# Waits at the edges of a TensorE-bound kernel: load order, warm-up matmuls, halved products, copies on ScalarE, group ends over two pairs

## The chip, the cores and the metric

The kernel runs on one core of a Trainium2 chip. The metric is the device time of one execution in microseconds (us), as the median of several.

The engines are TensorE (PE, matmuls), VectorE (DVE), ScalarE (ACT), GpSimd (POOL) and SyncE (SP, which here only issues DMA). In the lines of a profile, L342 is line 342 of that kernel's source, so one statement has different numbers in different kernels. `a<-b` is output from input. A matmul of the source appears as two instructions.

## The reference

Two layers of a compressed interaction network over x of shape (4096, 32, 16), each followed by a batch norm over rows and embedding:

```python
def _cin_layer(out, x, W, b, gamma, beta):
    r, _, e = x.shape
    h = jnp.einsum('rne,rfe->rnfe', out, x).reshape(r, -1, e)
    h = jnp.einsum('rce,oc->roe', h, W) + b[None, :, None]
    return _batchnorm(h, gamma, beta)
h1 = _cin_layer(x, x, W1, b1, g1, beta1)          # 1024 -> 128 channels
out, direct1 = (h1[:, :64], h1[:, 64:])
direct2 = _cin_layer(out, x, W2, b2, g2, beta2)   # 2048 -> 128 channels
return jnp.concatenate([direct1, direct2], axis=1).sum(axis=-1)
```

## The kernel before

Layer 1 goes over 128 tiles of 512 columns. VectorE multiplies `a` and `b` of a tile to `z`, TensorE multiplies `z` by the weights in four matmuls. The diagonal leftovers (`zr`) of four tiles come in four matmuls ahead of them. ScalarE takes the sums out of PSUM (the memory that the matmuls write), and VectorE collects their statistics.

```python
for t in range(NT):
    s = t % GROUP
    if s == 0:
        r = load_rem(t // GROUP)
        zr = rpool.tile([P, T], FP, tag="zr", name="zr")
        nc.vector.tensor_tensor(zr, r[:, :T], r[:, T:], ALU.mult)
    a, b = load_main(t)
    z = zpool.tile([P, 2, 2, T], FP, tag="z", name="z")
    nc.vector.tensor_tensor(z, ...)
    ...
    with tc.issue_after(loads[-1].ins):
        for first, load in EARLY:      # x loads, differences, first loads of layer 2
            if t == first:
                early.append(load())
```

Layer 2 goes over 64 pairs of tiles, each in four stages: one ordinary stage first (16 matmuls), then three that use Strassen's scheme (14 matmuls each, at the price of additions on the operands). VectorE makes two products `zz` per stage, GpSimd forms the operands `t` of the Strassen stages in two operations, and the sums of a pair are combined during the next pair. After 20 pairs the statistics of a group are aggregated. The direct half of layer 1's output is scaled during the first pair:

```python
def write_direct():
    sum_direct(NC - 1)
    ...
    nc.vector.tensor_scalar(ss1[high, 2:3], ss1[high, 1:2], float(EMB), None, ALU.mult)
    for half in range(2):
        nc.vector.tensor_copy(direct[half * KEEP : (half + 1) * KEEP, :], ss1[high, 0:3:2])
    nc.scalar.activation(d1, d1, AF.Identity, scale=direct[:, 0:1], bias=direct[:, 1:2])
...
# in combine, which runs during the next pair:
    if idle:
        dve(idle.pop(0))
    add(e[:, 0], both, x62)
    ...
    if stats_x.ended():
        ends = [swap_groups, stats_y.aggregate]
        if c < NC - 1:
            idle[:0] = [lambda: [end() for end in ends][-1]]
```

Of the kernel before, what the change touches and what calls it, by code (L numbers as in the profile page):

```python
# [35 lines left out]
FP = mybir.dt.float32  # L36
AF = mybir.ActivationFunctionType
# [3 lines left out]
P = 128  # L41
# [13 lines left out]
PLAIN = 3  # L55
STAGES = (3, 0, 1, 2)
DIFF = 16


@with_exitstack  # L60
def tile_cin(ctx: ExitStack, tc: tile.TileContext, xa, xb, xr, w1, w1m, w2, bn, out):
# [2 lines left out]
    const = ctx.enter_context(tc.tile_pool(name="const", bufs=1))  # L64
    dram = ctx.enter_context(tc.tile_pool(name="dram", bufs=1, space=bass.MemoryType.DRAM))
    sums = ctx.enter_context(tc.tile_pool(name="sums", bufs=1))
    spool = ctx.enter_context(tc.tile_pool(name="spool", bufs=1))
    epool = ctx.enter_context(tc.tile_pool(name="epool", bufs=2))
    xpool = ctx.enter_context(tc.tile_pool(name="xpool", bufs=1))
    bpool = ctx.enter_context(tc.tile_pool(name="bpool", bufs=2))  # L70
# [15 lines left out]
    class Stats:  # L86
# [25 lines left out]
        def ended(self):  # L112
            return self.at == self.sizes[self.group]

        def aggregate(self):

            size = self.sizes[self.group]
            group = self.groups[:, self.group]
            stats = self.stats[:, :size].rearrange("p a b -> p (a b)")
            done = nc.vector.bn_aggr(group[:, 1:3], stats)  # L120
            if size != LAST:
                done = nc.vector.tensor_scalar(group[:, 2:3], group[:, 2:3], size / LAST, None, ALU.mult)
            self.at = 0
            self.group += 1
            return done

    def scale_shift(name, groups, gamma, beta, factor=None):

# [75 lines left out]
        return dict(zip(STAGES, a)), b, bx  # L204



    select = bpool.tile([KEEP, 4, 16, 8], FP, tag="b", name="select")
    nc.gpsimd.memset(select, 1.0)
# [19 lines left out]
    with ExitStack() as one:  # L229
# [6 lines left out]
        def load_rem(g):  # L236

            r = rpool.tile([P, 2 * T], FP, tag="r", name="r")
            nc.sync.dma_start(r, bass.AP(xr.tensor, xr.offset + g * P * 2 * T, [[2 * T, P], [1, 2 * T]]))
            return r  # L240

        def load_main(t):
# [8 lines left out]

        w1_sb = wpool.tile([P, 6, P], FP, tag="w1", name="w1_sb")
        nc.scalar.dma_start(w1_sb, w1)
        w1m_sb = lpool.tile([P, 6, P], FP, tag="a", name="w1m_sb")
        nc.scalar.dma_start(w1m_sb, w1m)
        bn_sb = load_bn()
        w2_sb = const.tile([P, 16, P], FP, tag="w2", name="w2_sb")
        s_sb = const.tile([P, 4, 4, 2, KEEP], FP, tag="s", name="s_sb")
        neg_sb = const.tile([P, 2, 2, KEEP], FP, tag="neg", name="neg_sb")
        nc.scalar.dma_start(w2_sb, w2)  # L260
        b1, g1, beta1, b2, g2, beta2 = (bn_sb[:, k : k + 1] for k in range(6))
        nc.vector.tensor_tensor(w1_sb, w1_sb, w1m_sb, ALU.add)

# [19 lines left out]
        def finish(t):  # L283

            c, half = divmod(t, 2)
            ps = pss.pop(t)
            to = slice(half * KEEP, (half + 1) * KEEP)
            if half == 0:
                eds[c] = epool.tile([P, T], FP, tag="ed", name="ed")
                kept[c] = opool.tile([KEEP, 2 * T], FP, tag="h", name="kept")  # L290
            ed = eds[c]
            if t == NT - 1:
                stats1.add(ps, b1)
            else:
                e = opool.tile([P, T], FP, tag="e", name="e")
                nc.scalar.activation(e, ps, AF.Identity, bias=b1)  # L296
                stats1.add(e)
            if stats1.ended():
                stats1.aggregate()
            h = kept[c]  # L300
            nc.scalar.activation(h[:, half * T : (half + 1) * T], ps[:KEEP, :], AF.Identity, bias=b1[:KEEP])
            if half == 1:
                nc.scalar.dma_start(hs[c], kept.pop(c))
            if t == NT - 1:
                return ps
            evict_direct(ed[to, :], ps)
            if half == 1:
                sum_direct(c)
# [9 lines left out]
                ALU.add,  # L318
            )

        zr = None
        for t in range(NT):
            s = t % GROUP
            if s == 0:
                r = load_rem(t // GROUP)
                zr = rpool.tile([P, T], FP, tag="zr", name="zr")
                nc.vector.tensor_tensor(zr, r[:, :T], r[:, T:], ALU.mult)
            a, b = load_main(t)
            z = zpool.tile([P, 2, 2, T], FP, tag="z", name="z")
            nc.vector.tensor_tensor(  # L330
                z,
                a.rearrange("p (a t) -> p a t", a=2).unsqueeze(2).to_broadcast([P, 2, 2, T]),
                b.rearrange("p (b t) -> p b t", b=2).unsqueeze(1).to_broadcast([P, 2, 2, T]),
                ALU.mult,
            )
            if s % 4 == 0:
                for k in range(4):
                    ps = pss[t + k] = psum.tile([P, T], FP, tag="ps", name="ps")
                    rows = slice(32 * k, 32 * (k + 1))
                    nc.tensor.matmul(ps, w1_sb[rows, 4 + s // 4, :], zr[rows, :], start=True, stop=False)  # L340
            for m in range(4):
                nc.tensor.matmul(pss[t], w1_sb[:, m, :], z[:, m // 2, m % 2, :], start=False, stop=(m == 3))  # L342
            if t > 0:
                finish(t - 1)
            if t == 8:
                combine_weights()
            with tc.issue_after(loads[-1].ins):
                for first, load in EARLY:
                    if t == first:
                        early.append(load())  # L350
# [4 lines left out]
    def keep_running(count):  # L355

        for k in range(count):
            nc.tensor.matmul(  # L358
                running, w2_sb[:, k, :], w2_sb[:, 0:4, :].rearrange("p a b -> p (a b)"), start=True, stop=True
            )  # L360
# [13 lines left out]
    nc.tensor.matmul(keep_ps, spread, blocks, start=True, stop=True)  # L374
    keep = const.tile([P, 4, 2], FP, tag="keep", name="keep")
    nc.vector.tensor_copy(keep, keep_ps)
    keep_running(2)

    with tc.issue_after(root1):
        evict_direct(eds[NC - 1][high, :], last)  # L380
# [1 line left out]
    def write_direct():  # L382
        sum_direct(NC - 1)
        direct = const.tile([P, 2], FP, tag="direct", name="direct")
        nc.vector.tensor_scalar(ss1[high, 2:3], ss1[high, 1:2], float(EMB), None, ALU.mult)
        for half in range(2):
            nc.vector.tensor_copy(direct[half * KEEP : (half + 1) * KEEP, :], ss1[high, 0:3:2])
        nc.scalar.activation(d1, d1, AF.Identity, scale=direct[:, 0:1], bias=direct[:, 1:2])
        for half in range(2):
            nc.scalar.dma_start(  # L390
                out[:KEEP, half * (ROWS // 2) : (half + 1) * (ROWS // 2)],
                d1[half * KEEP : (half + 1) * KEEP, :],
            )
# [8 lines left out]
    groups_of = -(-(NC - LAST) // SG) + 1  # L402
    groups2 = const.tile([P, 2, groups_of, 3], FP, tag="groups2", name="groups2")
    stats_x, stats_y = Stats("x", NC), Stats("y", NC, groups2[:, 0])

    def swap_groups():
        g = stats_x.group
        stats_x.aggregate()
        nc.vector.tensor_copy(groups2[low, 1, g], stats_x.groups[high, g])
        return nc.vector.tensor_copy(groups2[high, 1, g], stats_x.groups[low, g])  # L410

    b2_swapped = const.tile([P, 1], FP, tag="b2s", name="b2_swapped")
    nc.vector.tensor_copy(b2_swapped[low], b2[high])


    idle = []
    lasts = {}

    def queue(engine, make):
# [5 lines left out]
    def dve(make):  # L425
        return queue("dve", make)
# [7 lines left out]
    def multiply(z, a, b):  # L434

        a = a.unsqueeze(1).unsqueeze(1).to_broadcast([P, 2, 2, T])
        dve(lambda: nc.vector.tensor_tensor(z, a, b.rearrange("p (k q) t -> p k q t", k=2), ALU.mult))  # L437

    def factor(a, i, half):
        f = factors.tile([P, T], FP, tag="f", name="f")  # L440
# [21 lines left out]
            queue("pe", lambda: nc.tensor.matmul(self.of[x], w, b, start=start, stop=stop))  # L462

    def ordinary(sums_, z):
        for k in range(4):
            q = k % 2
            z1, z2 = z[:, 0 if k < 2 else 3, q], z[:, 2 if k < 2 else 1, q]
            a11, a21, a12, a22, s1, s2, s3, s4 = weights(PLAIN, q)
            sums_.matmul(3, s4 if k < 2 else neg_sb[:, 0, q], z2)
            sums_.matmul(2, a11 if k < 2 else a12, z1)  # L470
            sums_.matmul(5, s1 if k < 2 else neg_sb[:, 1, q], z2)
            sums_.matmul(4, a21 if k < 2 else a22, z1)
# [21 lines left out]
    def combine(c, sums_):  # L494
# [27 lines left out]
        dve(lambda: stats_x.add(e[:, 0]))  # L522
        dve(lambda: stats_y.add(e[:, 1]))
        if stats_x.ended():
            ends = [swap_groups, stats_y.aggregate]
            if c < NC - 1:
                idle[:0] = [lambda: [end() for end in ends][-1]]
            else:
                for end in ends:
                    dve(end)  # L530
        yield
        dve(
            lambda: nc.vector.tensor_reduce(
# [11 lines left out]
    for c in range(NC):  # L545
# [14 lines left out]
        for k, i in enumerate(STAGES):  # L560

            z = z2pool.tile([P, 4, 2, T], FP, tag="zz", name="zz")
            multiply(z[:, 0::3], f1, b)
            if k in (1, 2, 3):

                step()
            f2 = factor(raw[i], i, 1)
            if k == 1:
                step()
            multiply(z[:, 1:3], f2, bx)  # L570
            if k == 1:
                step()
            if k == 2:
                step()
            if k < 3:
                f1 = factor(raw[STAGES[k + 1]], STAGES[k + 1], 0)
            if k == 0:
                step(2)
            if k == 1:
                step()  # L580
            if i == PLAIN:
                ordinary(sums_, z)
            else:
                strassen(sums_, i, z, k == 3)
            if c == 0 and k == 1:
                with tc.issue_after(lasts["dve"].ins), tc.issue_after(lasts["act"].ins):
                    write_direct()
# [89 lines left out]
```

## Time and profile before

| | kernel before |
|---|---|
| time at hand for the prediction, median of 3 | 2136.95 us (2136.57 to 2137.31) |
| span of the profiled execution | 2135.7 us |
| TensorE busy | 98% |
| VectorE busy | 90% |
| first layer, 4 tiles, steady | 15.00 us |
| second layer, a pair, at best | 24.89 us |

With TensorE busy in all but 2% of the span, the page as a whole tells little. One reads the timelines of single stretches, from one matmul start to the next: 0.43 us is the fastest pace of the full matmuls (kernel before, from 19.17 us on), at which the array is called warm here, and 0.85 the pace of a cold one (there from 14.31 to 18.58 us). The prediction shows these lines.

### The profile page before, as it was taken

How to read it: one execution, taken by the hardware profiler on the slowest of the kernel's cores; microseconds unless marked ns; L12 is line 12 of the kernel's file. 1: busy time of each engine (PE TensorE's matmuls, PEld its weight loads, DVE VectorE, ACT ScalarE, POOL GpSimd, SP SyncE). 2: the span in 40 equal slices, each digit the busy share in tenths (PEclk: the TensorE clock that was granted, in tenths of full speed). 3: DMA queues.
4: the chain of work that ended last, by engine and by line, in shares of the span. 5: the costliest groups of instructions: out<-in, count | busy, mean ns of one | idle time of the engine just before them, and what ended most of it. 6: DMA issues, size and time to landing. Idle time of an engine off the chain costs nothing.

```text
span 2135.7 us, 23411 instructions
## 1 busy us (share of the span) xinstructions
PE 2091.2 (98%) x8716; PEld 733.8 (34%) x8716; DVE 1916.1 (90%) x1465; ACT 853.8 (40%) x1221; POOL 1328.5 (62%) x390
## 2 busy tenths in 40 slices
PE   7999999998999999999999999999999999999996
PEld 3344444443333333333333333333333333333332
DVE  7888888897999999989999998999999989999996
ACT  3555555554333333333333333333333333433332
POOL 0000000003878888887888888878888888788885
PEclk9999999999999999999999999999999999999998
DMA  9999999997767677777677777766667777666751
GB/s 355 332 341 335 333 338 351 356 353 197 189 166 171 167 185 175 171 173 171 158 175 180 174 172 173 174 166 159 167 169 173 172 174 174 163 166 160 171 135 40
DMA packets 112019, 440.65 MB, mean 206 GB/s; under 512 B 13088, under 2 KB 13088, under 8 KB 103456
## 3 DMA queue, kind: packets, MB, share of 16 engines
q1 hardware_dynamic: 105152, 416.33, 71.5%
q10 hardware_dynamic: 6752, 22.81, 2.9%
q8 instruction: 68, 1.11, 0.2%
q14 instruction: 47, 0.39, 0.1%
HBM read 417.07 MB, written 22.02 MB: 206 GB/s over the span
## 4 chain that ended last, share of the span: by engine, by line
PE 83%; POOL 8%; DVE 4%; issue 2%; DMA 2%; ACT 1%; SPq 0%; DVEq 0%; POOLq 0%
PE x L462 63%; PE ps L342 18%; POOL t L481 5%; POOL t L478 3%; DVE zz L437 2%; PE ps L340 1%; DVE z L330 1%; DMA b<-in_xb 1%; ACT both L429 0%; DMA x<-in_xb 0%; DMA a<-in_xa 0%; DMA r<-in_xr 0%; DVE e L432 0%; PE running L358 0%; DVE x L184 0%
## 5 line engine op out<-in xcount | busy, mean ns | idle before, releaser
L462 PE MATMUL x<-zz,w_sb 128*64 128x512 f32 x2560 | 968.9, 593 | 0.0
L478 POOL TENSOR_TENSOR t<-zz 128x1024 f32<-128x1024 f32 x192 | 456.8, 2379 | 770.7 <-DVE zz L437 770.7
L462 PE MATMUL x<-zz,s_sb 128*64 128x512 f32 x2048 | 924.8, 594 | 4.6 <-issue 4.6
L481 POOL TENSOR_TENSOR t<-zz,t 128x2048 f32<-128x2048 f32 x192 | 875.8, 4562 | 15.1
L462 PE MATMUL x<-t,s_sb 128*64 128x512 f32 x1536 | 696.4, 594 | 6.7 <-POOL t L481 6.5
L429 ACT ACTIVATE f<-a,keep 128x512 f32<-128x512 f32 x512 | 398.2, 778 | 634.0 <-DVE zz L437 631.3
L437 DVE TENSOR_TENSOR zz<-f,b 128x2048 f32<-128x2048 f32 x256 | 582.8, 2277 | 0.9 <-ACT f L429 0.8
L437 DVE TENSOR_TENSOR zz<-f,bx 128x2048 f32<-128x2048 f32 x256 | 582.5, 2275 | 0.1
L342 PE MATMUL ps<-z,w_sb 128*128 128x512 f32 x1024 | 451.1, 598 | 6.6 <-DVE z L330 6.6
L462 PEld LDWEIGHTS x<-zz,s_sb 128*64 128x64 f32 x2048 | 281.1, 137 | 372.0 <-issue 356.9
L462 PE MATMUL x<-t,w_sb 128*64 128x512 f32 x768 | 363.2, 595 | 0.0
L462 PEld LDWEIGHTS x<-t,s_sb 128*64 128x64 f32 x1536 | 205.1, 137 | 456.8 <-issue 397.5
L330 DVE TENSOR_TENSOR z<-a,b 128x2048 f32<-128x2048 f32 x128 | 292.9, 2288 | 56.7 <-DMA b<-in_xb 30.9
L462 PEld LDWEIGHTS x<-zz,w_sb 128*64 128x64 f32 x2560 | 301.3, 137 | 109.6 <-issue 106.4
L342 PEld LDWEIGHTS ps<-z,w_sb 128*128 128x128 f32 x1024 | 192.8, 191 | 263.4 <-issue 241.3
L462 PE MATMUL x<-zz,neg_sb 128*64 128x512 f32 x512 | 230.2, 592 | 0.0
L296 ACT ACTIVATE e<-ps,bn_sb 128x512 f32<-128x512 f32 x127 | 87.3, 688 | 245.7 <-PE ps L342 227.4
L432 DVE TENSOR_TENSOR both<-both,x 128x512 f32<-128x512 f32 x64 | 44.0, 688 | 130.4 <-ACT both L429 130.4
L429 ACT ACTIVATE u<-e,bn_sb 64x512 f32<-64x512 f32 x64 | 46.2, 722 | 192.3 <-DVE e L432 192.3
L462 PEld LDWEIGHTS x<-zz,neg_sb 128*64 128x64 f32 x512 | 70.1, 137 | 146.3 <-issue 146.3
L462 PEld LDWEIGHTS x<-t,w_sb 128*64 128x64 f32 x768 | 99.9, 137 | 0.0
L429 ACT ACTIVATE both<-x 64x512 f32<-64x512 f32 x64 | 38.1, 595 | 138.6 <-PE x L462 138.6
(70 smaller groups left out, 878.3 us busy)
## 6 DMA issues: line engine op xcount, KB each, us to landing
a<-h SPq DMA_DIRECT2D x256, 512.0 KB, 5.1
b<-in_xb SPq DMA_DIRECT2D x128, 512.0 KB, 6.9
a<-in_xa SPq DMA_DIRECT2D x128, 512.0 KB, 6.1
b<-in_xb SPq DMA_DIRECT2D x64, 1024.0 KB, 7.1
bx<-in_xb SPq DMA_DIRECT2D x64, 512.0 KB, 6.0
bx<-x SPq DMA_DIRECT2D x64, 512.0 KB, 7.7
h<-kept ACTq DMA_DIRECT2D x64, 256.0 KB, 5.6
r<-in_xr SPq DMA_DIRECT2D x16, 512.0 KB, 7.7
```

The lines of the kernel that those rows point to most:

```text
L296: nc.scalar.activation(e, ps, AF.Identity, bias=b1)
L330: nc.vector.tensor_tensor(z, a.rearrange("p (a t) -> p a t", a=2).unsqueeze(2).to_broadcast([P, 2, 2, T]), b.rearrange("p (b t) -> p b t", ...
L340: nc.tensor.matmul(ps, w1_sb[rows, 4 + s // 4, :], zr[rows, :], start=True, stop=False)
L342: nc.tensor.matmul(pss[t], w1_sb[:, m, :], z[:, m // 2, m % 2, :], start=False, stop=(m == 3))
L429: return queue("act", lambda: nc.scalar.activation(to, source, AF.Identity, **scale_bias))
L432: return dve(lambda: nc.vector.tensor_tensor(to, x, y, ALU.add))
L437: dve(lambda: nc.vector.tensor_tensor(z, a, b.rearrange("p (k q) t -> p k q t", k=2), ALU.mult))
L462: queue("pe", lambda: nc.tensor.matmul(self.of[x], w, b, start=start, stop=stop))
L478: queue("pool", lambda: nc.gpsimd.tensor_tensor(t2, t3, b11, ALU.add))
L481: queue("pool", lambda: nc.gpsimd.tensor_tensor(t[:, 1:3], z[:, 2:4], twice, ALU.subtract))
```

## The change

The intent is to take time out of the edges. At the start: the first tile's operands are loaded ahead of the leftovers' `r`, the 1 MB of w2 leaves the start, and six dummy matmuls warm the array up. In layer 1 the early work is ordered behind the product of its own tile. In layer 2 the first pair's ordinary products are made in halves, with more dummies ahead of them; the small copies move to ScalarE; and a group end is spread over two pairs. The core of the diff:

```diff
-    spool = ctx.enter_context(tc.tile_pool(name="spool", bufs=1))
+    spool = ctx.enter_context(tc.tile_pool(name="spool", bufs=2))
...
+    ones = epool.tile([P, T], FP, tag="ed", name="ones")
+    nc.vector.memset(ones, 1.0)
+    begun = factors.tile([P, T], FP, tag="f", name="begun")
+    for _ in range(BEGIN):                      # BEGIN = 6
+        nc.tensor.matmul(begun, ones[:, :P], ones, start=True, stop=True)
...
-        nc.scalar.dma_start(w2_sb, w2)
...
-        zr = None
+        main = [load_main(0)]
+        r = load_rem(0)
         for t in range(NT):
...
+            if s == 4 and t + 4 < NT:
+                r = load_rem(t // GROUP + 1)
+            if t + 1 < NT:
+                main.append(load_main(t + 1))
...
-            if t == 8:
+            if t == 20:
                 combine_weights()
-            with tc.issue_after(loads[-1].ins):
+            with tc.issue_after(loads[-1].ins), tc.issue_after(product.ins):
+                if t == 6:
+                    nc.sync.dma_start(w2_sb, w2)
...
-    keep_running(2)
+    keep_running(4)
...
-        nc.vector.tensor_scalar(ss1[high, 2:3], ss1[high, 1:2], float(EMB), None, ALU.mult)
         for half in range(2):
-            nc.vector.tensor_copy(direct[half * KEEP : (half + 1) * KEEP, :], ss1[high, 0:3:2])
+            for k, factor in enumerate((1.0, float(EMB))):
+                to = direct[half * KEEP : (half + 1) * KEEP, k : k + 1]
+                nc.scalar.activation(to, ss1[high, k : k + 1], AF.Identity, scale=factor)
...
-        for k in range(4):
+        for k in (0, 2, 1, 3):                  # ordinary(): q = k % 2
...
-            ends = [swap_groups, stats_y.aggregate]
+            g = stats_x.group
+            ends = [stats_x.close(), stats_y.close()]
             if c < NC - 1:
-                idle[:0] = [lambda: [end() for end in ends][-1]]
+                swaps.append(g)                 # swapped on ScalarE when idle is empty
+                idle[:0] = ends
...
+            if c == k == 0:
+                f2 = factor(raw[i], i, 1)
+                for q in range(2):
+                    multiply_part(z[:, 0::3], f1, b, q)
+                    multiply_part(z[:, 1:3], f2, bx, q)
```

More of the change, by code (lines that the diff above doesn't have):

```diff
@@ L57 @@
 DIFF = 16
+BEGIN = 6
 @with_exitstack
@@ L113, in ended, with close, aggregate @@
             return self.at == self.sizes[self.group]
-        def aggregate(self):
-            size = self.sizes[self.group]
+        def close(self):
+            size, stats = self.sizes[self.group], self.stats
             group = self.groups[:, self.group]
-            stats = self.stats[:, :size].rearrange("p a b -> p (a b)")
-            done = nc.vector.bn_aggr(group[:, 1:3], stats)
-            if size != LAST:
-                done = nc.vector.tensor_scalar(group[:, 2:3], group[:, 2:3], size / LAST, None, ALU.mult)
             self.at = 0
             self.group += 1
-            return done
+            def aggregate():
+                done = nc.vector.bn_aggr(group[:, 1:3], stats[:, :size].rearrange("p a b -> p (a b)"))
+                if size != LAST:
+                    done = nc.vector.tensor_scalar(group[:, 2:3], group[:, 2:3], size / LAST, None, ALU.mult)
+                return done
+            return aggregate
     def scale_shift(name, groups, gamma, beta, factor=None):
@@ L238, in load_rem @@
             r = rpool.tile([P, 2 * T], FP, tag="r", name="r")
-            nc.sync.dma_start(r, bass.AP(xr.tensor, xr.offset + g * P * 2 * T, [[2 * T, P], [1, 2 * T]]))
+            with tc.issue_after(loads[-1].ins) if loads else nullcontext():
+                nc.sync.dma_start(r, bass.AP(xr.tensor, xr.offset + g * P * 2 * T, [[2 * T, P], [1, 2 * T]]))
             return r
@@ L253, in tile_cin @@
         nc.scalar.dma_start(w1_sb, w1)
-        w1m_sb = lpool.tile([P, 6, P], FP, tag="a", name="w1m_sb")
+        w1m_sb = zpool.tile([P, 6, P], FP, tag="z", name="w1m_sb")
         nc.scalar.dma_start(w1m_sb, w1m)
@@ L298, in finish @@
             if stats1.ended():
-                stats1.aggregate()
+                stats1.close()()
             h = kept[c]
@@ L324, in tile_cin @@
             if s == 0:
-                r = load_rem(t // GROUP)
                 zr = rpool.tile([P, T], FP, tag="zr", name="zr")
                 nc.vector.tensor_tensor(zr, r[:, :T], r[:, T:], ALU.mult)
-            a, b = load_main(t)
+            if s == 4 and t + 4 < NT:
+                r = load_rem(t // GROUP + 1)
+            if t + 1 < NT:
+                main.append(load_main(t + 1))
+            a, b = main.pop(0)
             z = zpool.tile([P, 2, 2, T], FP, tag="z", name="z")
-            nc.vector.tensor_tensor(
+            product = nc.vector.tensor_tensor(
                 z,
@@ L404, in tile_cin, with swap_group @@
     stats_x, stats_y = Stats("x", NC), Stats("y", NC, groups2[:, 0])
-    def swap_groups():
-        g = stats_x.group
-        stats_x.aggregate()
-        nc.vector.tensor_copy(groups2[low, 1, g], stats_x.groups[high, g])
-        return nc.vector.tensor_copy(groups2[high, 1, g], stats_x.groups[low, g])
+    for g, size in enumerate(stats_x.sizes):
+        nc.vector.memset(groups2[:, 1, g, 0:1], size / LAST)
+    def swap_group(g):
+        for x, y in ((low, high), (high, low)):
+            last = nc.scalar.activation(groups2[x, 1, g, 1:3], stats_x.groups[y, g, 1:3], AF.Identity)
+        return last
     b2_swapped = const.tile([P, 1], FP, tag="b2s", name="b2_swapped")
     nc.vector.tensor_copy(b2_swapped[low], b2[high])
-    idle = []
+    idle, swaps = [], []
     lasts = {}
@@ L437, in multiply, with multiply_part @@
         dve(lambda: nc.vector.tensor_tensor(z, a, b.rearrange("p (k q) t -> p k q t", k=2), ALU.mult))
+    def multiply_part(z, a, b, q):
+        a = a.unsqueeze(1).to_broadcast([P, 2, T])
+        dve(lambda: nc.vector.tensor_tensor(z[:, :, q], a, b.rearrange("p (k q) t -> p k q t", k=2)[:, :, q], ALU.mult))
     def factor(a, i, half):
@@ L524, in combine @@
         if stats_x.ended():
-            ends = [swap_groups, stats_y.aggregate]
+            g = stats_x.group
+            ends = [stats_x.close(), stats_y.close()]
             if c < NC - 1:
-                idle[:0] = [lambda: [end() for end in ends][-1]]
-            else:
-                for end in ends:
-                    dve(end)
+                swaps.append(g)
+                idle[:0] = ends
+            else:
+                dve(ends[0])
+                queue("act", lambda: swap_group(g))
+                dve(ends[1])
+        elif swaps and not idle:
+            g = swaps.pop()
+            queue("act", lambda: swap_group(g))
         yield
@@ L562, in tile_cin @@
             z = z2pool.tile([P, 4, 2, T], FP, tag="zz", name="zz")
-            multiply(z[:, 0::3], f1, b)
+            if c == k == 0:
[3 more added lines that the diff above has]
+                    multiply_part(z[:, 1:3], f2, bx, q)
+            else:
+                multiply(z[:, 0::3], f1, b)
             if k in (1, 2, 3):
                 step()
-            f2 = factor(raw[i], i, 1)
-            if k == 1:
-                step()
-            multiply(z[:, 1:3], f2, bx)
+            if c > 0 or k > 0:
+                f2 = factor(raw[i], i, 1)
+                if k == 1:
+                    step()
+                multiply(z[:, 1:3], f2, bx)
             if k == 1:
```

## The prediction

Passages are cut from it where marked: statements about the hardware that no trace shows. No term of the sum goes with them: it is 3.5 + 3.3 + 2.5 + 1.7 = 11.0 us as before. In the paragraph ahead of the parts, "it" is the array.

> **What bounds the kernel now.** I read the page first: busy time by engine, then the chain that ended last.
>
> ```profile
> PE 2091.2 (98%) x8716; PEld 733.8 (34%) x8716; DVE 1916.1 (90%) x1465; ACT 853.8 (40%) x1221; POOL 1328.5 (62%) x390
> ...
> PE 83%; POOL 8%; DVE 4%; issue 2%; DMA 2%; ACT 1%; SPq 0%; DVEq 0%; POOLq 0%
> ```
>
> TensorE (PE) is the bound of both layers, and the change removes none of its work. In the steady part of the first layer four tiles take 15.00 us on the chain (1.07 + 13.93), so 32 such groups are 480.1 us. In the second layer a pair takes at best 24.89 us from first matmul to first matmul, 1593.0 us for 64. Together 2073.1 of the 2135.7 us span. All that can be won lies in the other 62.6 us, so I looked for the places where TensorE starts late, runs slowly or waits. There are four.
>
> *The start.* Timeline of TensorE:
>
> ```profile
> 7.81 2.09 PE L340 MATMUL ps<-zr,w_sb 32*128 32x512 f32 x8 [7.81 <-DVE w_sb L262]
> 13.29 16.76 PE L342 MATMUL ps<-z,w_sb 128*128 128x512 f32 x32 [3.40 <-DVE z L330]
> ```
>
> Eight leftover matmuls, then 3.40 us of idling until the first full product is there; it waited for `a` of tile 0, third on its queue, which landed at 10.86. The first full matmuls also start 0.85 us apart, up to about 18.6; from 19.17 on it is 0.43. So the array is slow for nearly 6 us.
>
> *The stall at 71 to 75 us.* Timeline of VectorE (DVE):
>
> ```profile
> 71.11 1.43 DVE L184 TENSOR_TENSOR x<-x 128x256 f32<-128x256 f32 x4 [6.35 <-DMA x<-in_xb]
> 72.46 2.28 DVE L330 TENSOR_TENSOR z<-a,b 128x2048 f32<-128x2048 f32 x1
> ```
>
> The four differences, meant for tiles 34 to 40, stand in VectorE's order before the product of tile 15, and their operand came late. That product ends at 74.74 and its matmul starts at 74.80, 3.76 us after the one before instead of 0.43: 3.33 us lost.
>
> *The first pair of layer 2.* Timeline of GpSimd (POOL), and one line of VectorE's:
>
> ```profile
> 512.45 2.36 POOL L478 TENSOR_TENSOR t<-zz 128x1024 f32<-128x1024 f32 x1 [509.97 <-DVE zz L437]
> 514.89 4.54 POOL L481 TENSOR_TENSOR t<-zz,t 128x2048 f32<-128x2048 f32 x1
> 522.03 2.38 POOL L478 TENSOR_TENSOR t<-zz 128x1024 f32<-128x1024 f32 x1 [2.61 <-DVE zz L437]
> ```
>
> ```profile
> 515.42 4.21 DVE L387 COPY direct<-ss 64x2 f32<-64x2 f32 x2
> ```
>
> Two copies of 64x2 take 4.21 us; the other copies of this size take 0.16. The first ends with GpSimd's operation (519.43). Behind it stands the product that GpSimd needs next, so GpSimd idles 2.61 us. TensorE starts this pair at 508.02, cold until 513.93, and waits for `t` at 529.11 and 536.06 (starts 1.43 and 1.31 us apart). The pair takes 29.81 us.
>
> *Group ends.* Timeline of VectorE, pair 21:
>
> ```profile
> 1036.70 0.69 DVE L120 BATCH_NORM_AGGREGATE groupsx<-statsx 128x2 f32<-128x120 f32 x1
> 1037.30 0.64 DVE L120 BATCH_NORM_AGGREGATE groups<-statsy 128x2 f32<-128x120 f32 x1
> ...
> 1038.04 0.68 DVE L432 TENSOR_TENSOR e<-both,x 128x512 f32<-128x512 f32 x1
> 1038.75 0.16 DVE L409 COPY groups<-groupsx 64x3 f32<-64x3 f32 x1
> 1038.93 0.16 DVE L410 COPY groups<-groupsx 64x3 f32<-64x3 f32 x1
> 1039.12 2.29 DVE L437 TENSOR_TENSOR zz<-f,bx 128x2048 f32<-128x2048 f32 x1
> ```
>
> Without the group end the add would start at 1036.70 and the product 0.60 later; it starts 1.82 us later than that. GpSimd waits for that product, and its three rounds of 6.98 us have little room in 24.9. Pairs 21, 41 and 61 take 26.53, 26.80 and 26.76 us against some 24.95 for the mean pair.
>
> [...] 0.85 against 0.43 us between starts; the idling of 4.59 us before 508.02 made it cold, that of 3.3 at 71 did not. [...] In the trace `r`, first on one queue, and `w1`, first on the other, both issued at 0.81, landed at 5.10 and 5.31.
>
> **The change part by part.**
>
> 1. Start. The order becomes a, b, r on SyncE's queue, and w2 (1 MB) leaves ScalarE's. Today the first 512 KB of SyncE's queue landed at 5.10, the second (`b`) at 7.69. So a and b of tile 0 should both be there at about 7.7. VectorE then does the product (2.29), the weight sum (0.96) and zr (0.69), in this order in the built program; consecutive operations overlap by 0.08, so zr ends at about 7.75 + 2.29 + 0.88 + 0.61 = 11.5. r, third, has no w2 beside it and should land near 9. The leftover matmuls run warm, 1.07 instead of 2.09, and tile 0's full ones from 12.6 in 8 x 0.43 = 3.43 us. Tile 1 then begins at about 16.05, not 19.60: **3.5 us won**. Its product: the two reductions (1.01 + 0.67, to 13.1), then 2.29, so 15.4: in time. The warm array needs the six dummies: 12 instructions from about 1.4 us, some 6 at 0.85 and 6 at 0.43, to about 9; the gap to 11.5 is shorter than the 3.3 us that kept the clock today.
> 2. The differences now stand behind the product of tile 33 or so in VectorE's built order, and w2's sums behind tile 7's: **3.3 us won**, unless the loads fall behind.
> 3. First pair. The halves bring the first matmul from 508.02 to 503.43 + 2 x 1.13 + 0.1 = 505.8 (on today's scale), and three dummies behind keep_ps keep the array warm: on TensorE alone 2.2 + 2.9 us. But GpSimd starts once the fourth full product is done, at 512.3, and halving does not move that (it adds about 0.1). Then 3 x 6.98 us without a break: 512.45 + 20.95 = 533.4, after which the last 1.71 us of matmuls follow: 535.15. Today the last wait ended at 536.06. So the halves and dummies win about nothing, and moving the copies away wins the idle 2.61: **2.5 us**. ScalarE has 1.4 us gaps here, for four copies of an estimated 0.2 (table's ACTIVATE of 128x1: 0.20).
> 4. Group ends. The first of the two pairs gets an aggregate and its dependent scaling, 0.69 + about 0.10, so 0.78 us in place of 1.82; the second the same. Four differences of 0.33 in pairs 4 to 7 added 0.70 in all above 24.95, so a pair swallows some 0.2. Today 1.82 - 0.2 = 1.6 (observed 1.6 to 1.85); after, 2 x (0.78 - 0.2) = 1.15. Three group ends: **1.7 us** with the observed cost. At the very end two copies (0.36 us) leave VectorE, two ACTIVATEs run beside the second aggregate: 0.
>
> Sum: 3.5 + 3.3 + 2.5 + 1.7 = 11.0; 2136.95 - 11.0 = 2125.95.
>
> **The rivals.** *The first pair is bound by TensorE:* then the halves and the warm array would count nearly in full, the pair ending at 505.8 + 24.9 = 530.7 instead of 535.15: 4.4 us more, near 2121.5. Against it: both waits for `t` today end with GpSimd's operation, and its chain does not start earlier. *The array goes cold again between the dummies and tile 0:* nearly 2.9 of the 3.5 us of the start are gone, about 2129. [...] *The loads take over:* the DMA engines are at 1.00 to 1.02 of their time from 30 to 60 us, and w2 now comes in there. A stall at tiles 8 to 18 gives back up to 3.3 us: 2129. Against it: products were ready 4 to 5.5 us ahead of TensorE at tiles 6 to 14 although two x loads came in between. *The group ends are swallowed whole*, as each half is small: 1.7 becomes 5, near 2122.5.
>
> **Range and chances.** The terms are uncertain by about 1.5 (start), 1 (stall), 1 (pair) and 1.5 us (group ends): together some 2.6, so 3.5 to 4 either side holds eight in ten. Runs of the kernel before differ by 0.7 us. 2% is 42.7 us: far more than all the slack (62.6) lets this change win, and nothing in it adds work of such size. Faster 0.01, within 2% 0.98, slower 0.01.
>
> **What would show it right or wrong.** First full matmul near 12.6 and 0.43 apart; no gap of 3.3 us between matmuls near 70 us; last matmul of layer 1 about 6.8 us earlier. In the first pair GpSimd's six operations without a gap, the first matmul warm and some 2.2 us earlier against the end of layer 1, and TensorE waiting 2 to 3 us for `t`. Group-end pairs near 25.5 twice instead of 26.7 once. I am wrong if TensorE's first pair ends more than 1 us off, if matmuls at the start are 0.85 apart, or if a wait for `b` stops TensorE in the first 80 us.

## The result, and the profile after

The changed kernel takes 2128.79 us, the median of four runs from 2127.44 to 2129.99; the kernel before took 2137.13 us beside it (2136.57 to 2137.91). The ratio is 0.9961, with a 95% interval of 0.9943 to 0.9978. A ratio is the mean time of one kernel's fast runs over that of the other's in the same rounds, so it is not quite the ratio of the medians. The gain is 8.3 us, of 11 forecast.

The page of the changed kernel, busy times and chain:

```profile
PE 2094.9 (99%) x8732; PEld 736.7 (35%) x8732; DVE 1912.0 (90%) x1461; ACT 855.6 (40%) x1233; POOL 1328.7 (63%) x390
...
PE 85%; POOL 9%; DVE 3%; issue 2%; ACT 1%; DMA 0%; DVEq 0%; SPq 0%; POOLq 0%
```

DMA went from 2% of the chain to 0%: the chain of layer 1 leads back through no load but the first `b`. The rest is read by stretches, cut at four matmul starts: tile 1's first matmul, the last of layer 1, the first of pair 1, the last of all.

| stretch, us | before | after | won | forecast |
|---|---|---|---|---|
| start to tile 1 | 19.60 | 18.35 | 1.25 | 3.5 |
| tile 1 to the end of layer 1 | 478.42 | 474.92 | 3.50 | 3.3 |
| end of layer 1 to pair 1 | 39.82 | 37.29 | 2.53 | 2.5 |
| pair 1 to the last matmul | 1578.43 | 1575.76 | 2.67 | 1.7 |
| tail | 19.45 | 19.40 | 0.05 | 0 |

That is 10.0 us between the two profiled executions, 1.7 more than between the medians: the one after was the fastest of its four (2127.44 us), the one before (2137.44) 0.3 us above its median.

Timeline of TensorE at the start, changed kernel (columns: start, duration, engine, line, operation, tiles, count, and in brackets the idle time before it with what ended it):

```profile
1.55 7.50 PE L215 MATMUL begun<-ones 128*128 128x512 f32 x12 [1.55 <-DVE ones L212]
12.09 1.64 PE L355 MATMUL ps<-zr,w_sb 32*128 32x512 f32 x8 [3.04 <-DVE zr L338]
13.65 15.16 PE L357 MATMUL ps<-z,w_sb 128*128 128x512 f32 x32
```

The dummies end at 9.05, as forecast, and the leftovers start at 12.09. But the eight leftovers take 1.64 us, not 1.07, and the first full matmuls come 1.02, 0.85 and 0.68 us apart: the array has gone cold again. It did so not in the 3.04 us between, but at work: in the packed trace the fifth leftover starts 0.52 us after the fourth, as in a warm run (0.51 in `begin9b`), and the next step, from the eighth to the first full matmul, takes the cold 0.99. (Where the array is cold from the first one on, as in `best3`, both steps take 0.99.)

Timeline of VectorE near the old stall, changed kernel:

```profile
65.18 2.29 DVE L345 TENSOR_TENSOR z<-a,b 128x2048 f32<-128x2048 f32 x1
67.38 0.69 DVE L106 BATCH_NORM_STATS2 stats<-e 128x6 f32<-128x512 f32 x1
67.99 2.27 DVE L345 TENSOR_TENSOR z<-a,b 128x2048 f32<-128x2048 f32 x1
```

These are the products of tiles 15 and 16. No difference of x stands between them; the differences run one by one from 137 us on, and no matmul of layer 1 waits. Product 15 is there 2.75 us before TensorE wants it, where it was 0.06.

Timelines of the first pair of layer 2, changed kernel, GpSimd and one matmul of TensorE:

```profile
507.83 2.38 POOL L502 TENSOR_TENSOR t<-zz 128x1024 f32<-128x1024 f32 x1 [505.35 <-DVE zz L456]
510.29 4.53 POOL L505 TENSOR_TENSOR t<-zz,t 128x2048 f32<-128x2048 f32 x1
514.77 2.37 POOL L502 TENSOR_TENSOR t<-zz 128x1024 f32<-128x1024 f32 x1
```

```profile
514.87 0.64 PE L486 MATMUL x<-t,s_sb 128*64 128x512 f32 x1 [2.36 <-POOL t L505]
```

GpSimd's third operation follows the second at once. TensorE, which started this pair warm at 501.14 (starts 0.43 to 0.45 us apart), then waits 2.36 us for `t` (forecast 2 to 3) and twice more after that (0.74 and 0.72): it is early for nothing.

Timeline of VectorE at the second group end, changed kernel, pairs 41 and 42:

```profile
1530.39 0.69 DVE L124 BATCH_NORM_AGGREGATE groupsx<-statsx 128x2 f32<-128x120 f32 x1
1531.11 0.15 DVE L126 TENSOR_SCALAR groupsx<-groupsx 128x1 f32<-128x1 f32 x1
1531.18 0.68 DVE L451 TENSOR_TENSOR e<-both,x 128x512 f32<-128x512 f32 x1
...
1555.38 0.69 DVE L124 BATCH_NORM_AGGREGATE groups<-statsy 128x2 f32<-128x120 f32 x1
1556.10 0.15 DVE L126 TENSOR_SCALAR groups<-groups 128x1 f32<-128x1 f32 x1
1556.17 0.68 DVE L451 TENSOR_TENSOR e<-both,x 128x512 f32<-128x512 f32 x1
```

Each half delays the add by 0.79 us, as forecast. But pair 41 takes 25.72 us and pair 42 25.00, an ordinary length (half of all pairs take 24.96 or less): the second half costs about nothing.

### The profile page after: what moved, and what is told of

It is laid out like the page before. It is cut to its first block, busy times and chain, and to the rows that moved or that the text cites. A ratio compares the mean times of both kernels' runs of the same rounds, so it can differ in the third digit from the quotient of the medians.

```text
span 2125.7 us, 23431 instructions
## 1 busy us (share of the span) xinstructions
PE 2094.9 (99%) x8732; PEld 736.7 (35%) x8732; DVE 1912.0 (90%) x1461; ACT 855.6 (40%) x1233; POOL 1328.7 (63%) x390
## 4 chain that ended last, share of the span: by engine, by line
PE 85%; POOL 9%; DVE 3%; issue 2%; ACT 1%; DMA 0%; DVEq 0%; SPq 0%; POOLq 0%
PE x L486 62%; PE ps L357 21%; POOL t L505 5%; POOL t L502 3%; PE ps L355 2%; DVE zz L456 2%; ACT both L448 1%; DVE e L451 0%; DMA b<-in_xb 0%; DVE zz L461 0%; PE running L375 0%; DVE x L188 0%; DVE d L647 0%; ACT u L448 0%; DVE groupsx L124 0%
## 5 line engine op out<-in xcount | busy, mean ns | idle before, releaser
L486 PE MATMUL x<-zz,neg_sb 128*64 128x512 f32 x512 | 240.6, 592 | 0.0
```

What stands on the lines that cost most here:

```text
L486: queue("pe", lambda: nc.tensor.matmul(self.of[x], w, b, start=start, stop=stop))
```

## The experiments

My theory after the result: the differences' order and the copies gave what was forecast; the halves gave nothing, because GpSimd binds the first pair; the start lost most of its gain to the cold array; and the second half of a group end is swallowed. The rivals are in the expectations. The stretches of all usable traces, in us:

| kernel | start to tile 1 | rest of layer 1 | to pair 1 | to the last matmul | time, median |
|---|---|---|---|---|---|
| begin0 | 19.71 | 475.06 | 37.26 | 1575.71 | 2129.17 |
| whole | 18.29 | 474.92 | 37.16 | 1575.53 | 2128.77 |
| dvecopies | 20.40 | 477.31 | 39.88 | 1575.67 | 2132.59 |
| anchor (before, with one part) | 18.67 | 476.88 | 39.77 | 1578.30 | 2135.00 |
| apart | 20.22 | 474.92 | 37.29 | 1577.60 | 2130.41 |
| together | 19.00 | 476.70 | 37.28 | 1576.85 | 2130.10 |
| begin9b | 17.58 | 479.35 | 37.30 | 1575.73 | 2130.30 |
| addondve | 19.77 | 474.92 | 36.56 | 1575.93 | 2128.48 |
| best2 | 16.96 | 474.92 | 36.55 | 1576.09 | 2125.92 |
| best3 | 19.94 | 474.92 | 36.55 | 1576.12 | 2126.32 |

The last two stretches repeat to 0.2 us wherever the code of layer 2 is the same; the first two vary from run to run. The kernel before had medians of 2136.09, 2139.17, 2137.53 and 2138.02 us in the four jobs, so times are compared within a job.

**begin9: nine dummies.**

```diff
-BEGIN = 6
+BEGIN = 9
```

> The changed kernel with nine warm-up matmuls instead of six. Theory: the array went cold again because the dummies ended at 9.05 us and the first leftover matmul came at 12.09; three more warm dummies of 0.86 us end at about 11.6, the idling falls from 3.0 to about 0.5 us, and all matmuls of tile 0 run 0.43 us apart. Tile 1's first matmul then comes at about 16.6 instead of 18.35 us, the kernel takes about 2126.5 us and its runs lie within 1 us of each other, not 2.5. Rival: [...] tile 1 stays near 18.3 us and the spread stays.

Its profiled execution took 4543 us, with matmuls at half the rate from first to last (those of layer 1 take 1.15 us on the mean, 0.60 in the changed kernel); the other four took 2127.26 to 2128.74. The spread was 1.5 us, but the median of these four is 2128.17, not 2126.5. Nothing is shown of the start, so it was run again.

**begin9b: the same kernel.**

> The same kernel as begin9 once more, because its profiled execution ran at half the matmul rate from end to end (4543 us, one of five executions, the other four 2127.3 to 2128.7) and so shows nothing of the start. Expected as there: dummies end at about 11.6 us, tile 0 warm, tile 1's first matmul near 16.6 us and a time near 2126.5; by the rival 18.3 us and no gain. A second execution at half rate would mean that more dummies provoke it; none would leave it a rare event of unknown cause.

```profile
1.55 9.56 PE L215 MATMUL begun<-ones 128*128 128x512 f32 x18 [1.55 <-DVE ones L212]
12.97 1.14 PE L355 MATMUL ps<-zr,w_sb 32*128 32x512 f32 x8 [1.86 <-DVE zr L338]
```

After 1.86 us of idling the array is still warm: the eight leftovers take 1.14 us, and tile 1 begins 4.61 us after the first of them (6.26 in the changed kernel). It came at 17.58 and not 16.6, because VectorE finished `zr` 0.9 us later in this run. The time did not fall at all (2130.3), and the trace says where it went: layer 1 from tile 1 on took 479.35 us, 4.4 more than without waits. The first matmuls of tiles 7 and 14, at 41.41 and 69.36 us, came 2.39 and 1.70 us after the ones before. Timeline of VectorE ahead of the first of them:

```profile
37.26 1.29 DVE L287 TENSOR_TENSOR s_sb<-w_sb 128x512 f32<-128x512 f32 x2 [1.42 <-DMA w_sb<-in_w]
38.47 0.69 DVE L287 TENSOR_TENSOR s_sb<-s_sb,w_sb 128x512 f32<-128x512 f32 x1
39.07 2.29 DVE L345 TENSOR_TENSOR z<-a,b 128x2048 f32<-128x2048 f32 x1
```

The weight sums of w2 stand ahead of tile 7's product in VectorE's order and wait for w2, 1 MB loaded just then (27.77 to 37.23 us). This is a wait that the change put there; in the profiled execution of the changed kernel, where the sums stand ahead of tile 8's product, w2 was in time. The second one follows waits for b (2.02 and 2.41 us). Both rivals of the forecast have happened, though not in one run.

**begin0: no dummies.**

```diff
-BEGIN = 6
+BEGIN = 0
```

> The changed kernel without any warm-up matmul, so what is left at the start is the order of the loads. Theory: leftovers from 12.1 us at 0.85 us pace (about 2.1 us), then cold full matmuls for some 4 us: tile 1 begins at about 19.3 us, 1 us later than with six dummies and hardly before the 19.60 of the kernel before. Rival: the six dummies bought nothing; tile 1 stays at 18.35 us. Layer 2 as in the changed kernel either way.

Tile 1 began at 19.71 us. Here `zr` came 1.07 us later than in the changed kernel, so measured from the leftovers' start it is 6.55 against 6.26 us: the six dummies bought 0.3 us in this pair of traces, less than the theory's 1. In all six usable traces with these six dummies in the place of the changed kernel (the changed kernel, `whole`, `together`, `addondve`, `apart`, `dvecopies`) it took 6.15 to 7.57 us, on the mean 6.85; warm it is 4.61 (`begin9b`). As far as these traces tell, with one that has no dummies, six are no better than none.

**whole: the first pair's products whole, two dummies.**

```diff
-    keep_running(4)
+    keep_running(2)
-        for k in (0, 2, 1, 3):
+        for k in range(4):
-            if c == k == 0:
-                ... (products by halves)
-            else:
-                multiply(z[:, 0::3], f1, b)
+            multiply(z[:, 0::3], f1, b)
```

> The changed kernel with the first pair's products whole again, the old order of the ordinary matmuls, and two dummies instead of four. Theory (GpSimd binds the first pair): the first matmul of layer 2 comes 2.3 us later and cold, but the pair ends at the same time against the end of layer 1 within 0.3 us (36.7 us from the last matmul start of layer 1 to that of pair 1, in the changed kernel 37.3), because GpSimd's six operations start 0.1 to 0.2 us earlier. Rival (TensorE binds): the pair ends 2 to 5 us later and the kernel takes 2131 to 2134 us.

Timelines of TensorE and GpSimd, each with its first operation of layer 2:

```profile
503.22 0.82 PE L486 MATMUL x<-zz,s_sb 128*64 128x512 f32 x1 [4.59 <-issue]
507.65 2.38 POOL L502 TENSOR_TENSOR t<-zz 128x1024 f32<-128x1024 f32 x1 [505.17 <-DVE zz L456]
```

The first matmul of layer 2 came 10.01 us after the last of layer 1, not 7.87, and was slower (0.82 us, 0.61 in the changed kernel); yet pair 1 began 37.16 us after it, 0.13 sooner than with the halves. TensorE does not bind this pair. The rival is out.

**dvecopies: the copies of the direct half on VectorE.**

```diff
-            for k, factor in enumerate((1.0, float(EMB))):
-                ...
-                nc.scalar.activation(to, ss1[high, k : k + 1], AF.Identity, scale=factor)
+        nc.vector.tensor_scalar(ss1[high, 2:3], ss1[high, 1:2], float(EMB), None, ALU.mult)
+            nc.vector.tensor_copy(direct[half * KEEP : (half + 1) * KEEP, :], ss1[high, 0:3:2])
```

> The changed kernel with the copies for the direct half back on VectorE. Theory (a copy of 64x2 is shut out by GpSimd's operation): the first of the two copies takes about 4 us and ends with GpSimd's operation, GpSimd then idles about 2.6 us before its third operation, and the first pair takes 2.5 us longer (31.9 against 29.42 us); the kernel about 2131.3 us. Rival: with products ordered by halves the copy falls at another moment or its wait is hidden behind the 1.2 us that VectorE idles anyway, and the pair takes less than 1 us longer.

Timelines of VectorE and GpSimd:

```profile
515.25 4.18 DVE L404 COPY direct<-ss 64x2 f32<-64x2 f32 x2
```

```profile
514.72 4.51 POOL L504 TENSOR_TENSOR t<-zz,t 128x2048 f32<-128x2048 f32 x1
521.83 2.36 POOL L501 TENSOR_TENSOR t<-zz 128x1024 f32<-128x1024 f32 x1 [2.61 <-DVE zz L455]
```

The 2.61 us are back, to the digit, and the stretch to pair 1 grew by 2.59. This part is settled. (The median is 3.4 and 3.8 us above those of `begin0` and `whole` in the same job. The profiled execution, the slowest of the four, also waited for `b` near 325 us in layer 1; whether the others did has no trace.)

**anchor: the kernel before, with the early work ordered behind its tile's product.**

```diff
-            nc.vector.tensor_tensor(
+            product = nc.vector.tensor_tensor(
-            with tc.issue_after(loads[-1].ins):
+            with tc.issue_after(loads[-1].ins), tc.issue_after(product.ins):
```

> The kernel before with one part of the change alone: whatever is issued early in layer 1 (loads, differences) is ordered behind the product of its own tile. Theory: the 3.33 us gap between matmuls near 75 us is gone and nothing else moves, so the stretch from tile 1's first matmul to the last of layer 1 falls from 478.42 to about 475.0 us and the kernel takes about 3.4 us less, 2133 us. Rival: the loads were behind at that point anyway, and a wait for b stops TensorE within the next tiles; then the stretch stays above 477 us.

Timeline of TensorE:

```profile
60.14 14.00 PE L342 MATMUL ps<-z,w_sb 128*128 128x512 f32 x32
74.07 1.14 PE L340 MATMUL ps<-zr,w_sb 32*128 32x512 f32 x8
```

The gap near 75 us is gone. The stretch fell only to 476.88, between theory and rival, because matmuls waited 0.33, 0.44 and 0.87 us near 326, 353 and 387 us: there VectorE waits for `b`, and I take it that this is because the first loads of layer 2 come on top: an estimate, from `dvecopies`, where two of them are issued at 308.04 and 308.68 us and VectorE waits 4.14 us for `b` up to 323.01. Without these three it would be 475.24. `together` and `dvecopies` show such waits near 325 us too, other runs of the same code none. So the part is worth 3.2 to 3.5 us by the traces, and layer 1 has waits of up to 2.4 us in some executions. The times alone do not prove it: the ratio to the kernel before is 0.9986, with an interval of 0.9972 to 1.0001.

**together: both aggregates in one pair, swaps on ScalarE.**

```diff
-                idle[:0] = ends
+                idle[:0] = [lambda: [end() for end in ends][-1]]
```

> The changed kernel with both aggregates of a group end in one pair again, the swaps still on ScalarE. Theory: VectorE's delay is then 1.34 us in one pair instead of 0.78 in each of two, of which a pair swallows some 0.1 to 0.2; group-end pairs take about 26.2 us and the stretch from pair 1 to the last matmul about 1577.2 us, 1.4 us more than in the changed kernel, 1.2 less than in the kernel before. Rival: moving the copies away was the whole gain and spreading nothing; the stretch stays at 1575.8 us.

The stretch is 1576.85, 1.09 above the changed kernel and 1.58 below the kernel before. So of 2.67 us won, moving the copies gave 1.6 and spreading 1.1. Pairs 41 and 61 took 26.33 and 26.23 us.

**apart: the second half two pairs after the first.**

```diff
-                idle[:0] = ends
+                idle[:0] = [ends[0], None, ends[1]]
-            dve(idle.pop(0))
+            make = idle.pop(0)
+            if make is not None:
+                dve(make)
```

> The changed kernel with the second half of each group end two pairs after the first instead of one. Theory: the wait that the first half causes comes at the end of its pair, after the matmuls that release the next pair's work, so the next pair has that wait as a lead and swallows the second half; two pairs later the lead is used up. So each half costs about 0.6 us on its own, and the stretch from pair 1 to the last matmul grows from 1575.76 by about 1.5 us (0.5 for each of three group ends). Rival: a second half is swallowed wherever it stands, because a pair has room for 0.7 us; the stretch stays within 0.3 us.

It gave a wrong result: with the empty entry in the queue the fourth difference of x (at 1157.37 us) came after these differences were stored (1141.91). Its times are used all the same: where its code is that of the changed kernel, so are its stretches (474.92 and 37.29 us). Pairs 41 and 43 took 25.79 and 25.81 us, 61 and 63 25.76 and 25.74, and the stretch is 1.84 longer. So a half that stands alone costs some 0.85 us, and one right behind another costs nothing. The rival is out: it is the neighbour that matters. The traces show the mechanism; here the changed kernel's timelines of VectorE and TensorE, with the add of `both` that opens a pair's chain, ahead of pairs 41 and 42, and the wait at the end of pair 41:

```profile
1527.59 0.69 DVE L451 TENSOR_TENSOR both<-both,x 128x512 f32<-128x512 f32 x1 [1.93 <-ACT both L448]
1552.57 0.69 DVE L451 TENSOR_TENSOR both<-both,x 128x512 f32<-128x512 f32 x1 [1.23 <-ACT both L448]
1555.25 0.64 PE L486 MATMUL x<-t,s_sb 128*64 128x512 f32 x1 [0.61 <-POOL t L505]
```

The wait for `t` falls on the last matmuls of pair 41, and what lets the next pair's chain begin, the sum x11, comes before them. So the next pair starts its chain with the length of that wait as a lead: the add comes 3.71 us before the first matmul of pair 41 (at 1531.30), but 4.44 us before that of pair 42 (1557.02), where the second half then uses the lead up. In `apart` pair 42 has this lead (4.51), and pair 43 no longer (3.61).

One more thing in this trace, by TensorE's timeline: after its first wait for `t` in the first pair the array was cold, though the wait was as long as in the changed kernel, where it stayed warm.

```profile
516.75 0.91 PE L486 MATMUL x<-t,s_sb 128*64 128x512 f32 x1 [2.36 <-POOL t L505]
517.46 1.06 PE L486 MATMUL x<-t,s_sb 128*64 128x512 f32 x1
518.31 1.06 PE L486 MATMUL x<-t,s_sb 128*64 128x512 f32 x1
```

The stretch to pair 1 was 37.29 us all the same.

**after2: the changed kernel again.**

> The changed kernel as it is, once more, so that the spread of its parts is seen on a second trace. Theory: three stretches repeat within 0.1 us (end of layer 1 to pair 1 37.3 us, pair 1 to the last matmul 1575.8, the tail 19.4), and what varies is the start (tile 1's first matmul between 18.3 and 20.4 us) and layer 1 from there (474.9 us plus 0 to 4 us of waits for loads). Rival: layer 2 varies too.

The profiled execution took 7955.59 us. Timeline of TensorE:

```profile
1.55 19.96 PE L215 MATMUL begun<-ones 128*128 128x512 f32 x12 [1.55 <-DVE ones L212]
```

Twelve instructions in 19.96 us are 1.66 each, a quarter of the warm rate, and so from the first one on to the end. The profile's granted clock says 1.000. VectorE and GpSimd were no slower than usual in `begin9`: a product took 2.29 us, GpSimd's longer operation 4.52. The rate was low before the dummies had run, so they can't have provoked it within this execution. The other four runs took 2126.02 to 2129.59 us. The expectation about the stretches is not tested by this trace; the table above tests it.

**addondve: the first pair's first `t` on VectorE.**

```diff
+        if early:                       # c == 0 and k == 1
+            add(t2, t3, b11)
+        else:
             queue("pool", lambda: nc.gpsimd.tensor_tensor(t2, t3, b11, ALU.add))
```

> The changed kernel with GpSimd's first operation of layer 2 (the sum t2 of the first pair's second stage, 2.38 us there) done by VectorE, which has both operands at hand (about 1.2 us). Theory: GpSimd's chain binds the first pair, so the pair ends sooner by what its chain starts sooner, less what VectorE's later products give back: the stretch from the end of layer 1 to pair 1 falls from 37.29 to about 36.2 to 36.6 us. Rival: the first pair is bound by VectorE's products; then the stretch grows by 1.2 us.

The stretch fell to 36.56, within what was expected. VectorE needed 1.23 us where GpSimd needs 2.38; after it GpSimd waits 0.28 us once for a later product. Shortening GpSimd's chain shortens the pair, which speeding TensorE up did not. In the time the 0.73 us do not show: the median is 2128.48, with a ratio of 0.9954 like that of the changed kernel's fast runs beside it.

**best2: a version meant to beat both.**

```diff
-BEGIN = 6
+BEGIN = 9
+            with tc.issue_after(weights_sum.ins) if t == 0 else nullcontext():
+                product = nc.vector.tensor_tensor(...)
-                if t == 6:
+                if t == 4:
+                    ... (the two reductions of the selector)
+                if t == 44:
                     nc.sync.dma_start(w2_sb, w2)
+                if t == 56:
+                    combine_weights()
-            if t == 20:
-                combine_weights()
... and addondve
```

> A version meant to beat both: the changed kernel with nine dummies, the weight sum ahead of tile 0's product and the two reductions of the selector later, w2 loaded at tile 44 instead of 6 (after the x loads, before those of layer 2), and VectorE's t2 in the first pair. Theory: the leftovers start at 11.2 to 12.2 us and warm, tile 1 at 15.7 to 16.7 us (2 to 3.5 us sooner than in the changed kernel); w2 no longer competes with the tiles while they have their least lead, so layer 1 from tile 1 stays near 475 us; the first pair 1 us shorter: about 2125 us, 3.5 us less than the changed kernel beside it. Rival: starting sooner only moves the wait to the loads (as in begin9b, 479.4 us from tile 1 on), and the time stays within 1.5 us of the changed kernel's.

It took 2125.92 us, from 2125.15 to 2126.24, with a ratio of 0.9943 (0.9929 to 0.9956); the fast runs of the changed kernel in the same job have 0.9954. That is 2.5 us less on the mean, where 3.5 were expected, and a spread of 1.1 us. Which of its parts gave how much of it no run separates. Tile 1 began at 16.96, with no idling at all before the leftovers: the dummies ended last.

**best3: best2 with seven dummies.**

```diff
-BEGIN = 9
+BEGIN = 7
```

> best2 with seven dummies instead of nine, alone in its job and so the first kernel on its chip, as begin9 and after2 were when they ran at half and at a quarter of the rate. In best2 zr was ready at 11.20 us but the nine dummies, cold for longer in that execution, held the array until 12.42. Theory: with seven the array is free by 9.5 to 10.8 us, the leftovers start at about 11.3 and the idling before them is too short for the clock to fall, so tile 1 begins at 15.8 to 16.3 us instead of 16.96 and the kernel takes 2124.5 to 2125.5 us. Rival: with the idling back, the clock falls in some executions, tile 1 spreads over 16 to 18 us and the median is no better than best2's 2125.92. If being first with dummies at the start is what provokes the low rate, the first execution shows it again; a normal one says nothing against it.

Six runs: 2124.74, 2124.82, 2124.97, and 2127.66, 2128.10, 2128.70. The profiled one is of the slower three. Timeline of TensorE:

```profile
1.55 7.94 PE L215 MATMUL begun<-ones 128*128 128x512 f32 x14 [1.55 <-DVE ones L212]
12.26 2.09 PE L354 MATMUL ps<-zr,w_sb 32*128 32x512 f32 x8 [2.77 <-DVE zr L336]
```

After 2.77 us of idling the eight leftovers take 2.09 us, the cold time, and tile 1 begins at 19.94. The rival was right, and said too little (tile 1 by 18 us); the median, 2126.32, is no better than that of `best2`. That the faster three are those in which the array stayed warm is likely, as they differ by about 3 us, but they have no trace. The first execution ran at the normal rate.

## Why the prediction was right or wrong

The time was inside the range, 2.8 us above the number, and every part went in the forecast direction. Point by point, in the order of its steps:

1. *Start, 3.5 us: wrong.* The step that failed is "the gap to 11.5 is shorter than the 3.3 us that kept the clock today". The gap was 3.04 us, as b landed at 8.17 instead of 7.7 us, and the clock was lost all the same, half a us into the leftovers; in `best3` it was lost after 2.77 us. One gap that had been survived was taken for a safe length (in the measure of the 3.04 it was 3.16 us). That "matmuls at the start are 0.85 apart" was one of the prediction's own signs of being wrong. The gain was 1.25 us in the profiled execution. Over the six traces that keep the changed kernel's start, tile 1 begins at 18.29 to 20.40 us, on the mean 19.34, against 19.60 and 18.67 in two with the old start: on the mean nothing. Of the 3.3 us by which that mean misses the forecast 16.05, 2.2 are the cold array (6.85 against 4.61 us from the first leftover), the forecast's rival, and 1.0 a later `zr` (12.49 against 11.5).
2. *Stall, 3.3 us: right.* 3.50 in the profiled execution, 3.2 for the part alone. The rival of the loads was right in part: some executions wait up to 2.4 us in layer 1, and 4.4 in `begin9b`, where w2 was late (with waits for `b` ahead of tile 14 too).
3. *First pair, 2.5 us: right in size and mechanism.* 2.53 measured. `whole` shows that halves and dummies give nothing (they cost 0.13), `dvecopies` that the copies are all of it, and `addondve` that GpSimd's chain is the bound. The rival of a pair bound by TensorE is out. (The working sets 535.15, the end of the pair, beside 536.06, the end of today's last wait. The like figure is 537.83, the start of pair 1: 2.68 us, which fits the 2.5.)
4. *Group ends, 1.7 us: mis-sized.* 2.67 measured. The term that failed is "the second the same": each half was forecast to cost 0.58 us, 1.15 together. The first cost 0.8 and the second, right behind it, about nothing. Two pairs further on it does cost its own 0.85 (`apart`). What was overlooked is the lead that the first half's wait gives to the next pair.

The tail changed by 0.05 us, as forecast. In sum: 1.25 + 3.50 + 2.53 + 2.67 + 0.05 = 10.0 in the best execution of four, 8.3 at the median. A start that wins nothing on the mean leaves 3.5 + 2.5 + 2.7 = 8.7. So the sum came as near as it did with some luck: the start was put 3.5 us too high and the group ends 1.0 too low.

The low rate of two whole executions stays open. Both were the first kernel of their job, in its profiled execution, and had dummies at the very start. All this holds of `best3` too, whose first execution was normal; `anchor`, first without dummies, was normal as well.

## What to carry to other kernels

When the busiest engine is at 98%, cut the trace into stretches between instants that every version has, and compare those: here the last two repeat to 0.2 us while times spread by 2.5. Speeding up the engine that is early in a stretch won nothing here (the changed kernel has the first matmul of layer 2 2.14 us earlier than `whole`, and pair 1 0.13 later); find the chain it waits for, here GpSimd's, and shorten that (`addondve`: 0.73 us). Warm-up matmuls kept the array warm here only where they reached up to the real ones or nearly so (`best2`, no idling; `begin9b`, 1.86 us). And of two unavoidable delays, one in each of two successive rounds cost less here than both in one round (`together`, 1.09 us more over three group ends) or a round between them (`apart`, 1.84 more), because the wait that the first causes (0.61 us in pair 41) falls behind the point that releases the next round.

## What the traces show of the array's pace, and of a copy beside GpSimd

- Idle gaps: the array was cold after 2.36 (`apart`, first pair) and 2.77 us (`best3`), while it stayed warm after 1.86 (`begin9b`), 2.36 (changed kernel, first pair) and 3.16 us (kernel before, at 71 us). After 3.04 us (changed kernel) it was still warm and fell half a us later, at work. From 2.36 to 3.16 us these traces show both outcomes.
- Clock record: the runs show whole executions at half (4543 us) and at a quarter (7955.59 us) of the matmul rate, with a granted clock of 1.000 in the record. It also says 1.00 for the first 20 us of the kernel before, where matmuls start 0.85 us apart. The pace between matmul starts is the better witness.
- A copy of 64x2, 0.16 us otherwise, took 4.03 us beside GpSimd's 4.54 us operation (kernel before) and cost the chain 2.61 us, twice to the digit (`dvecopies` again). A VectorE `tensor_scalar` of 64x1 ran in 0.15 us beside GpSimd's operation (kernel before, at 512.92).
